# The first tile of pairs prepared inside an earlier stage, and the last chunk's reciprocal applied when attention loads it

## The chip, the cores and the metric

The kernel runs on one core of a Trainium2 chip. The core has a tensor engine (PE; its weight loads are a row of their own, PEld), a vector engine (DVE), a scalar engine (ACT), GpSimd (POOL) and SyncE (SP), which only issues transfers. [...] Matmuls read SBUF and write PSUM, which this kernel uses in eight banks of 128 x 512 values. The metric is the device time of one execution in microseconds, given as the median of several runs.

## The reference

Four graph layers run one after the other on x of 8 batches, 2048 nodes and 64 features. Each layer normalises x, applies ReLU, computes something on the graph and adds it to x. Only layer 0 and the beginning of layer 1 matter here. Layer 0, cut to its core (E is 64 hyperedges, called edges below; H says which node belongs to which):

```python
h = x @ W
alpha = softmax(where(H.T > 0, leaky_relu(h @ a_node), NEG))     # per edge, over its nodes
agg = einsum('ben,bnf->bef', alpha, h)
beta = sigmoid((h @ a_gn)[:, None, :] + (agg @ a_ge)[:, :, None])
all_he = elu(beta * h[:, None] + (1 - beta) * agg[:, :, None])   # per (edge, node) pair
deg = maximum(adj.sum(-1), 1.0)[:, None]
industry = einsum('nm,bmf->bnf', adj / deg, x @ W_ind)
coefs1 = softmax(where(H > 0, attn_scores(elu(agg)), NEG))       # per node, over its edges
g = einsum('bne,benf->bnf', coefs1, all_he)
pair = stack([industry, g], axis=2)
out = einsum('bnk,bnkf->bnf', softmax(attn_scores(pair)), pair)
```

with `attn_scores(f) = tanh(f @ fcW + fcb) @ av`. Layers 1 to 3 (masked attention over neighbours, three message steps, and a graph convolution with a weight per node) follow and are not touched. H is sparse: a node has one edge and a few more, so the pairs (edge, node) of 128 nodes fit into 512 slots.

## The kernel before

Two batches of 64 features share the 128 partitions, so there are four batch pairs p (NP = 4). Nodes come in 16 tiles of 128 (NT) or in four chunks of 512 columns (NCW). A planner orders each engine's queue at compile time: it plays the program through with its own estimates of durations and issues an instruction on its engine when what it waits for is ready and no earlier traced one is ready too. What goes through the helper `InOrder` (the names V, A and G for DVE, ACT and POOL), or through `kit.mm` while `kit.strict` is set, keeps the order in which it was written. Everything else may be moved ahead, over long distances too. Pools of tiles are stacked in memory in the order in which their tags are first used, and a tile in a reused place waits for the last reader of what lay there.

The stages of layer 0 are these.

**Normalisation and lists** (to about 69 us). `norm` makes the normalised x, `pairs` makes for each node its first slot and its count (`mid`, `width`) and for each edge its ranks (Q), and Y is the normalised x times `W_ind`.

**Industries** (about 69 to 241 us), `industry(c)` for four chunks. Sixteen node tiles of adj are streamed, two in one load `at` of 512 KB issued by POOL into a pool of six buffers. PE multiplies them into four accumulators `acc0` to `acc3`, eight matmuls per node tile. After each node tile one function of the list `units` is called, so that small work is spread among the matmuls: for each of the 16 tiles `begin`, `part` and `end` of `members` (features `hi` and `lo` stored to DRAM, sums per edge into `pg` and `pd`), then `table_1` to `table_5` (tables per edge: `tab`, `ntab`, `etab`, and the denominators `rden`) and `rows` and `biases` (a bias table for layer 3). DVE adds the loads up (`ds`, L945). At a chunk's end DVE copies two accumulators and ACT two (`ev`, L949), PE sums `ds` over the partitions (`deg`, L952), DVE takes the minimum, clamps, inverts (L954 to L958) and multiplies the four `ev` by the reciprocal (L960), and SP stores them to `ind_dram` (L961). The units' PSUM tiles share two banks under the tag `ph`, and their SBUF tiles share four buffers under the tag `ev`.

**Pairs** (about 241 to 409 us), a loop over j = 0 to 70; a tile i has four steps k. Each tile is prepared by seven functions:

- `nodes`: ACT takes |slot - mid|, POOL compares it with `width` and so makes `sT` (which node has which slot)
- `ranks` and `edges`: PE makes `px`, DVE compares it with `slot` and makes `oT` (which edge has which slot)
- `turn` and `turned`: PE transposes `sT` into `pts`, ACT copies it to S
- `shares` and `shared`: PE makes `pm` with twelve small matmuls from `hhi`, `hlo` (the stored features, loaded by `features`) and `etab`, ACT makes `be` and `wt` from it

The loop prepares tile i + 1 while tile i is worked on; tile 0 is prepared before the loop, at L1236. A step then runs `pairs_of` (PE: `pd` and `pa`), `mixed` (two DVE operations, one exponential on ACT), `weighed` (DVE, then a multiplication on POOL) and `gathered` (PE adds the slots back to nodes with S). `divided`, `back` and `done` finish a tile into `gT`.

**Attention between industry and g** (about 409 to 492 us), a loop over 16 chunks (p, c). `first(i)` loads `iv` from `ind_dram` and scores it, `second(i)` scores g, `differ`, `third` and `fourth` weigh the two and add the result to x1. The first batch pair's sums stay on chip in `xs`, and `first_neighbours`, a generator that is advanced in this loop, begins layer 1 with them. The `iv` loads have nine buffers and are not held in order. The stores of g to x1, 1 MB each, go out on POOL as accumulating transfers (L1373).

Of the kernel before, what the change touches and what calls it, by code (L numbers as in the profile page):

```python
# [16 lines left out]
P = 128  # L17
# [744 lines left out]
def layer0(kit, hn, x1_dram, open_early, late_tile, between):  # L762
# [20 lines left out]

    sP = ExitStack()
# [10 lines left out]
    def features(i):  # L795

        hi = lst.tile([P, B * F + 2 * B], FR, tag="hhi", name="hhi", bufs=3)
        lo = lst.tile([P, B * F + 2 * B], FR, tag="hlo", name="hlo", bufs=3)
        nc.gpsimd.dma_start(out=hi, in_=hi_dram[i].bitcast(FR))
        nc.gpsimd.dma_start(out=lo, in_=lo_dram[i].bitcast(FR))  # L800
        return hi, lo

    with ExitStack() as sA:
# [110 lines left out]
        with ExitStack() as s1:  # L914
            sp = s1.enter_context(tc.tile_pool(name="streamf", bufs=6, reuse_waits="tile"))
# [10 lines left out]
            def industry(c):  # L926
# [20 lines left out]
                ev = [sb.tile([P, CW], FP, tag="ev", name="ev", bufs=4) for p in range(NP)]  # L947
                for p in range(NP):
                    (nc.scalar.copy if p % 2 else nc.vector.tensor_copy)(ev[p], acc[p])  # L949
# [3 lines left out]
                rdeg = sb.tile([P, CW], FP, tag="rdeg", name="rdeg", bufs=1)  # L953
# [4 lines left out]
                nc.vector.reciprocal(rdeg, rdeg)  # L958
                for p in range(NP):
                    nc.vector.tensor_mul(ev[p], ev[p], rdeg)  # L960
                    nc.sync.dma_start(out=ind_dram[p, :, cols(c)], in_=ev[p])  # L961

            def members(i):
# [14 lines left out]
                def part(j):  # L978
# [19 lines left out]
                    if j == 1:  # L998
                        nc.sync.dma_start(out=hi_dram[i], in_=hi.bitcast(FP))
                        nc.sync.dma_start(out=lo_dram[i], in_=lo.bitcast(FP))  # L1000

# [93 lines left out]
            for i in range(NT):  # L1095
                begin_, part_, end_ = members(i)
                units += [begin_, part_] + ([last] if last else [])
                last = end_
            units += [last, table_1]
            units += [lambda: rows(0), lambda: None, table_2, lambda: rows(1)]  # L1100
            for c, step in enumerate((table_3, table_4, table_5)):
                units += [lambda c=c: biases(c), step] + ([lambda c=c: rows(c + 2)] if c < 2 else [])
            units += [lambda: biases(3)]
# [4 lines left out]
        loaded = [features(i) for i in range(2)]  # L1108
# [5 lines left out]
    with ExitStack() as s0:  # L1114

        hot = s0.enter_context(tc.tile_pool(name="s_hot", bufs=2, reuse_waits="tile"))
# [7 lines left out]
        ident_r = sb.tile([P, P], FR, name="ident_r", bufs=1)  # L1124
        nc.vector.tensor_copy(ident_r, ident)
        tiles = [{} for i in range(NT)]

        def nodes(i):

            d = tiles[i]  # L1130
            d["sT"] = hot.tile([P, SLOTS], FR, tag="sT", name="sT", bufs=3)
            tmp = hot.tile([P, SLOTS], FP, tag="tmp", name="tmp", bufs=1)
            A.activation(tmp, slot, AF.Abs, bias=mid[:, i : i + 1])
            G.tensor_scalar(d["sT"], tmp, width[:, i : i + 1], None, op0=OP.is_lt)

        def ranks(i):
            d = tiles[i]
            d["px"] = ps.tile([P, SLOTS], FP, tag="px", name="px", bufs=2)
            mm(d["px"], Q[:, i].rearrange("p h e -> p (h e)"), d["sT"], start=True, stop=True)

        def edges(i):

            d = tiles[i]
            d["oT"] = hot.tile([P, SLOTS], FR, tag="oT", name="oT")
            V.tensor_tensor(d["oT"], d.pop("px"), slot, op=OP.is_equal)

        def turn(i):
            d = tiles[i]
            d["pt"] = ps.tile([P, NB, P], FP, tag="px", name="pts", bufs=2)
            for k in range(NB):  # L1150
                mm(d["pt"][:, k, :], d["sT"][:, k * P : (k + 1) * P], ident_r, start=True, stop=True)

        def turned(i):
            d = tiles[i]
            d["S"] = sb.tile([P, NB, P], FP, tag="S", name="S", bufs=3)
            A.activation(d["S"], d.pop("pt"), AF.Copy)

        def shares(i):

            d = tiles[i]  # L1160
            d["hi"], d["lo"] = loaded.pop(0)
            d["pm"] = pm = ps.tile([P, NB, 2 * B], FP, tag="px", name="pm", bufs=2)
            for k in range(NB):
                ks = slice(k * P, (k + 1) * P)
                mm(pm[:, k, :], d["sT"][:, ks], d["hi"][:, B * F :], start=True, stop=False)
                mm(pm[:, k, :], d["sT"][:, ks], d["lo"][:, B * F :], start=False, stop=False)
                mm(pm[:, k, :], d["oT"][:, ks], etab, start=False, stop=True)

        def shared(i):
            d = tiles[i]  # L1170
            d["be"] = sb.tile([P, NB, B], FP, tag="be", name="be")
            d["wt"] = sb.tile([P, NB, B], FP, tag="wt", name="wt")
            pm = d.pop("pm")
            A.activation(d["be"], pm[:, :, 0:B], AF.Tanh, scale=0.5)
            A.activation(d["wt"], pm[:, :, B:], AF.Copy)
# [60 lines left out]
        for step in (nodes, ranks, edges, turn, turned, shares, shared):  # L1236
            step(0)
        nodes(1)
# [6 lines left out]
        for j in range(last + 7):  # L1245
# [8 lines left out]
            if 3 <= j < last + 3:  # L1254
                weighed(j - 3)
            if 5 <= j < last + 5:
                gathered(j - 5)
# [35 lines left out]
    with ExitStack() as s0:  # L1293
# [17 lines left out]
        def first(i):  # L1311
# [3 lines left out]
            ths[i] = scores(iv, 2.0)  # L1315
# [30 lines left out]

        first(0)
# [8 lines left out]
        for i in range(len(chunks) + 2):  # L1356
# [12 lines left out]
            if i > 4:  # L1369
                next(steps, None)  # L1370
# [705 lines left out]
```

## Time and profile before

| what | us |
|---|---|
| median of three runs | 2058.82 |
| lowest and highest | 2055.77, 2061.78 |
| the profiled execution | 2053.27 |
| its span, from the first to the last instruction | 2051.2 |
| PE busy | 1992.0 (97%) |
| DVE busy | 1184.3 (58%) |
| ACT busy | 454.4 (22%) |
| POOL busy | 291.4 (14%) |

The profile is of one execution. Its times are counted from the start of the span. A line of a group or of the timeline names the line of the program, the engine, the operation and the tile that is written and read; L630 is the helper of everything that is kept in order on DVE, ACT and POOL, and L726 is that of `kit.mm`, so these are told apart by their tiles. The chain of waits goes back from the last instruction to what released it, and so on; "issue" in it is time in which the engine waited for nothing that the profile shows. An engine with a q behind it is its sequencer, which issues transfers. PE's ends are modelled, and some matmul records are missing. The clock is the share of full speed that PE was granted.

### The profile page before, as it was taken

The numbers are of one execution on the slowest core, as the hardware profiler recorded it, in microseconds if no ns is written. First come the engines' busy times: TensorE is split into PE (matmuls) and PEld (weight loads), VectorE is DVE, ScalarE is ACT, GpSimd is POOL, SyncE is SP. The second block draws the span as 40 slices with busy tenths as digits, with TensorE's granted clock in tenths as the row PEclk, the third lists the DMA queues.
The fourth block names the chain that finished last, engine by engine and source line by source line (L and its number), as shares of the span: only waits on it lengthen the run. The fifth ranks groups of instructions, "written<-read, shape, count | busy, mean of one in ns | idle before, by whom it ended". The sixth has DMA issues, their size and how long they took to land.

```text
span 2051.2 us, 23618 instructions
## 1 busy us (share of the span) xinstructions
PE 1992.0 (97%) x9164; PEld 1153.7 (56%) x9164; DVE 1184.3 (58%) x1867; ACT 454.4 (22%) x859; POOL 291.4 (14%) x399
## 2 busy tenths in 40 slices
PE   7999899988999999999999999999999999999997
PEld 4777677623323232237774567665477745677653
DVE  6667399866888888873216552245622165522355
ACT  4321255474111111121120111211111211112100
POOL 0211187511000000000001110101100011101012
PEclk9999899999999999999999999999999999999998
DMA  6766173185011111204101012100021001121000
GB/s 172 207 192 189 59 249 113 36 228 107 27 47 37 47 32 42 52 11 111 57 21 29 24 42 67 47 15 24 23 68 57 21 22 30 42 67 46 8 15 12
DMA packets 84251, 138.17 MB, mean 67 GB/s; under 512 B 32752, under 2 KB 33008, under 8 KB 81456
## 3 DMA queue, kind: packets, MB, share of 16 engines
q1 hardware_dynamic: 65200, 83.86, 13.9%
q0 software_dynamic: 18928, 52.70, 10.5%
q8 instruction: 74, 1.21, 0.3%
q14 instruction: 49, 0.40, 0.1%
HBM read 102.64 MB, written 37.03 MB: 68 GB/s over the span
## 4 chain that ended last, share of the span: by engine, by line
PE 71%; issue 15%; POOL 4%; DVE 3%; DMA 3%; ACT 2%; SPq 0%; POOLq 0%; DVEq 0%; ACTq 0%
PE acc L726 28%; PE o L726 11%; PE dn L726 6%; PE u L726 6%; PE pd L726 3%; PE acc L940 3%; PE pgs L726 2%; PE var L726 2%; PE mean L726 2%; PE py L726 2%; POOL fold L1964 1%; DMA iv<-ind_dram 1%; PE pm L726 1%; POOL ot L1965 1%; PE ph L726 1%
## 5 line engine op out<-in xcount | busy, mean ns | idle before, releaser
L726 PE MATMUL acc<-aT,parts 128*128 128x512 f32 x1664 | 456.0, 419 | 0.0
L726 PEld LDWEIGHTS acc<-aT,parts 128*128 128x128 f32 x1664 | 307.8, 188 | 111.8 <-issue 49.4
L1952 DVE TENSOR_TENSOR pr<-u,embf 128x512 f32<-128x512 f32 x256 | 170.6, 687 | 139.0 <-PE u L726 132.3
L1571 DVE SCALAR_TENSOR_TENSOR pt<-R,wd,aT 128x1024 f32<-128x1024 f32 x192 | 236.3, 1277 | 18.4 <-PE dn L726 6.6
L726 PE MATMUL u<-W3f,y 64*128 64x512 f32 x1024 | 241.0, 589 | 0.0
L726 PE MATMUL o<-pt,hS 128*64 128x512 f32 x1024 | 236.4, 599 | 0.8 <-DVE pt L1571 0.6
L726 PEld LDWEIGHTS u<-W3f,y 64*128 64x128 f32 x1024 | 99.2, 187 | 120.6 <-issue 120.6
L726 PEld LDWEIGHTS o<-pt,hS 128*64 128x64 f32 x1024 | 68.0, 136 | 159.2 <-issue 150.2
L726 PE MATMUL u<-W3f,v 64*128 64x512 f32 x512 | 138.8, 619 | 0.0
L940 PE MATMUL acc<-at,Y 128*128 128x512 f32 x512 | 134.9, 408 | 1.7 <-DVE ev L949 1.7
L1964 POOL TENSOR_TENSOR fold<-fold 128x256 f32<-128x256 f32 x64 | 47.8, 747 | 548.2 <-DVE fold L1963 510.4
L726 PE MATMUL dn<-pt,vd 128*32 128x512 f32 x1024 | 123.1, 598 | 0.0
L1788 DVE TENSOR_TENSOR yb<-py,cb_f 128x512 f32<-128x512 f32 x32 | 22.1, 691 | 173.8 <-PE py L726 173.8
L940 PEld LDWEIGHTS acc<-at,Y 128*128 128x128 f32 x512 | 94.2, 192 | 24.8 <-issue 4.1
L726 PE MATMUL acc<-aTl,parts 128*128 128x512 f32 x384 | 103.1, 405 | 0.0
L1956 DVE TENSOR_TENSOR pr<-pr 128x512 f32<-128x512 f32 x128 | 88.1, 688 | 2.2
L1571 DVE SCALAR_TENSOR_TENSOR pt<-R,wd,aTl 128x1024 f32<-128x1024 f32 x64 | 79.8, 1281 | 11.4 <-PE dn L726 8.2
L726 PEld LDWEIGHTS acc<-aTl,parts 128*128 128x128 f32 x384 | 72.2, 188 | 21.5 <-issue 5.7
L1856 POOL TENSOR_TENSOR bq<-bq,xp 128x512 f32<-128x512 f32 x16 | 20.6, 1285 | 434.0 <-DVE xp L1854 395.1
L1938 ACT COPY xs<-px 128x128 f32<-128x128 f32 x64 | 17.1, 267 | 272.7 <-POOL ot L1966 210.2
L630 POOL TENSOR_TENSOR mix<-ex,wt 128x512 f32<-128x512 f32 x64 | 68.3, 1069 | 33.7 <-DVE ex L630 28.9
L726 PEld LDWEIGHTS dn<-pt,vd 128*32 128x32 f32 x1024 | 26.7, 108 | 80.8 <-issue 75.4
(322 smaller groups left out, 2723.0 us busy)
## 6 DMA issues: line engine op xcount, KB each, us to landing
at<-in_adjT POOLq DMA_DIRECT2D x32, 512.0 KB, 4.5
raw<-in_adjT SPq DMA_DIRECT2D x64, 256.0 KB, 3.3
aT<-in_adjT POOLq DMA_DIRECT2D x12, 1024.0 KB, 5.3
xp<-xd SPq DMA_DIRECT2D x45, 256.0 KB, 3.2
R<-r_dram SPq DMA_DIRECT2D x14, 512.0 KB, 3.7
hi_dram<-hi SPq DMA_DIRECT2D x16, 264.0 KB, 2.5
lo_dram<-lo SPq DMA_DIRECT2D x16, 264.0 KB, 3.4
hhi<-hi_dram POOLq DMA_DIRECT2D x16, 264.0 KB, 3.1
```

The lines of the kernel that those rows point to most:

```text
L630: self.tc.keep_in_program_order(getattr(self.engine, name)(*args, **kw))
L726: one = self.nc.tensor.matmul(*args, **kw)
L940: mm(acc[p], Y[h][:, m, p, :], at[:, k, :], start=m + h == 0, stop=m == NT - 1 and h == 1)
L1571: nc.vector.scalar_tensor_tensor(pt, R[b2], wd[:, m, b2 : b2 + 1], aT[m][:, s].bitcast(FP), op0=OP.max, op1=OP.mult)
L1788: nc.vector.tensor_tensor(yb, py, bias[:, None, :].to_broadcast([P, 4, P]), op=OP.add)
L1856: nc.gpsimd.tensor_add(bq, bq, xp)
L1938: nc.scalar.copy(xs.rearrange("p h f -> p (h f)"), px)
L1952: nc.vector.tensor_tensor(a, u[h], emb[:, i, 8 * w : 8 * w + 8, None].to_broadcast([P, 8, F]), op=OP.mult)
L1956: nc.vector.tensor_add(pr[h], pr[h], a)
L1964: nc.gpsimd.tensor_add(fold[:, :, 0:2, :], fold[:, :, 0:2, :], fold[:, :, 2:4, :])
L1965: nc.gpsimd.tensor_add(ot, fold[:, :, 0, :], fold[:, :, 1, :])
```

## The change

Three things are done.

First, the preparation of tile 0 and `nodes(1)` become units of the last chunk's industries. The seven functions move up in the program, before the industries. They take engines, PSUM bank and scratch tile from a dictionary `now`: among the industries these are the plain engines (which the planner may reorder), the banks of `ph` and the buffers of `ev`; in the loop they are the ordered engines and the stage's own pools. The tiles of the first preparation (`sT0`, `oT0`, S0, `sT1`, `be0`, `wt0`) and `ident_r` lie in the pool `list`, the others in the stage's pool; `spot` chooses, and the number of buffers of each is as before. The `at` stream has four buffers instead of six. `features(0)` is traced in the units of tile 4.

Second, the last chunk (`late`) is no longer multiplied by its reciprocals at the chunk's end. All four of its accumulators are copied by ACT, and its clamped degrees stay in a new tile `rlast`, which all chunks now use. Steps 1 to 4 of the pairs each invert 128 of its columns.

Third, attention's loads get a function of their own, `fetched`, called for three chunks ahead of the loop and for chunk i + 3 at the end of step i. For the four pieces of the last chunk it multiplies `iv` by `rlast`, in order on DVE.

The diff, without the moved bodies that stay the same:

```diff
+    rlast = w0.tile([P, CW], FP, name="rlast")
...
+    ident_r = lst.tile([P, P], FR, name="ident_r")
+    nc.vector.tensor_copy(ident_r, ident)
+    tiles, loaded, now = [{} for i in range(NT)], [], {}
+
+    def spot(name, i, n, dt, bufs, ahead):
+        k = i % bufs
+        return (lst if k < ahead else now["pool"]).tile([P, n], dt, tag=f"{name}{k}", name=name)
+
+    def nodes(i):
+        d = tiles[i]
+        d["sT"] = spot("sT", i, SLOTS, FR, 3, 2)
+        tmp = now["tmp"]()
+        now["A"].activation(tmp, slot, AF.Abs, bias=mid[:, i : i + 1])
+        now["G"].tensor_scalar(d["sT"], tmp, width[:, i : i + 1], None, op0=OP.is_lt)
...
-            sp = s1.enter_context(tc.tile_pool(name="streamf", bufs=6, reuse_waits="tile"))
+            sp = s1.enter_context(tc.tile_pool(name="streamf", bufs=4, reuse_waits="tile"))
...
+                late = c == NCW - 1
                 for p in range(NP):
-                    (nc.scalar.copy if p % 2 else nc.vector.tensor_copy)(ev[p], acc[p])
+                    (nc.scalar.copy if late or p % 2 else nc.vector.tensor_copy)(ev[p], acc[p])
...
-                rdeg = sb.tile([P, CW], FP, tag="rdeg", name="rdeg", bufs=1)
+                rdeg = rlast
...
-                nc.vector.reciprocal(rdeg, rdeg)
+                if not late:
+                    nc.vector.reciprocal(rdeg, rdeg)
                 for p in range(NP):
-                    nc.vector.tensor_mul(ev[p], ev[p], rdeg)
+                    if not late:
+                        nc.vector.tensor_mul(ev[p], ev[p], rdeg)
                     nc.sync.dma_start(out=ind_dram[p, :, cols(c)], in_=ev[p])
...
+                    if j == 1 and i == 4:
+                        loaded.append(features(0))
...
+            now.update(
+                V=nc.vector, A=nc.scalar, G=nc.gpsimd,
+                tmp=lambda: sb.tile([P, SLOTS], FP, tag="ev", name="tmp", bufs=4),
+                bank=lambda shape, name: ps.tile(shape, FP, tag="ph", name=name, bufs=2),
+            )
...
             units += [last, table_1]
-            units += [lambda: rows(0), lambda: None, table_2, lambda: rows(1)]
-            for c, step in enumerate((table_3, table_4, table_5)):
-                units += [lambda c=c: biases(c), step] + ([lambda c=c: rows(c + 2)] if c < 2 else [])
-            units += [lambda: biases(3)]
+            units += [both((rows, 0), (nodes, 0)), both((ranks, 0), (turn, 0)), table_2]
+            units += [both((rows, 1), (edges, 0), (turned, 0))]
+            units += [both((biases, 0), (nodes, 1)), table_3, both((rows, 2))]
+            units += [both((biases, 1)), table_4, both((rows, 3))]
+            units += [both((biases, 2), (shares, 0)), table_5, both((biases, 3), (shared, 0))]
...
-        loaded = [features(i) for i in range(2)]
+        loaded.append(features(1))
...
-        hot = s0.enter_context(tc.tile_pool(name="s_hot", bufs=2, reuse_waits="tile"))
+        hot = s0.enter_context(tc.tile_pool(name="s_hot", bufs=1, reuse_waits="tile"))
...
+        now.update(
+            V=V, A=A, G=G, pool=hot,
+            tmp=lambda: hot.tile([P, SLOTS], FP, tag="tmp", name="tmp", bufs=1),
+            bank=lambda shape, name: ps.tile(shape, FP, tag="px", name=name, bufs=2),
+        )
...
-        for step in (nodes, ranks, edges, turn, turned, shares, shared):
-            step(0)
-        nodes(1)
...
+            if 1 <= j < 5:
+                part = slice((j - 1) * P, j * P)
+                V.reciprocal(rlast[:, part], rlast[:, part])
...
-        def first(i):
+        def fetched(i):
             p, c = chunks[i]
             iv = ivs[i] = io.tile([P, CW], FP, tag="iv", name="iv")
             nc.sync.dma_start(out=iv, in_=ind_dram[p, :, cols(c)])
-            ths[i] = scores(iv, 2.0)
+            if c == NCW - 1:
+                V.tensor_mul(iv, iv, rlast)
+
+        def first(i):
+            ths[i] = scores(ivs[i], 2.0)
...
+        for i in range(3):
+            fetched(i)
         first(0)
...
+            if i + 3 < len(chunks):
+                fetched(i + 3)
```

## The prediction

> **What bounds the kernel now.** I read the page first: PE is busy 97% of the span, so a stage gains only where PE stands or runs at half clock. Then the chain of waits around the two places that the change touches. First the end of the industries (start us, us, what):
>
> ```profile
> 240.65 0.47 PE deg L952 x2
> ...
> 241.83 0.60 DVE rdeg L957
> ...
> 242.49 3.32 DVE rdeg L958
> 245.81 0.56 DVE oT L630
> ...
> 246.41 2.31 PE pm L726 x10
> ...
> 249.74 1.57 POOL sT L630
> ```
>
> After the last industry matmul the chain leaves PE: the 3.3 us reciprocal stands in DVE's queue ahead of `oT` of tile 0, PE's `pm` waits for `oT`, and tile 1's `sT` is made only then. The first `pd` of the pairs starts at 248.56, 7.5 us after `deg`. The table by stretches (us; busy us and instructions of PE, PEld, DVE, ACT, POOL; clock; DMA share, GB/s) shows what follows:
>
> ```profile
> 241.00:245.40 4.40, 1.15 (x8) 0.87 (x7) 4.32 (x5) 1.53 (x3) 1.56 (x1) 1.00 0.00 0
> 245.40:255.70 10.30, 8.84 (x28) 7.14 (x29) 6.80 (x11) 2.95 (x7) 3.65 (x3) 0.50 0.27 102
> 255.70:273.00 17.30, 17.30 (x85) 12.83 (x83) 16.03 (x26) 7.61 (x15) 12.99 (x15) 1.00 0.78 244
> ```
>
> PE had 1.15 us of work in 4.4, and then ran 10.3 us at clock 0.50. From 255.7 on it is full.
>
> Second, the chain at the start of attention (380 to 450 us):
>
> ```profile
> 411.88 20.93 DMA iv<-ind_dram
> 432.81 0.14 issue
> 432.95 1.14 PE pf L726 x4
> ```
>
> PE and then DVE wait for one load of 256 KB that takes 20.9 us. SP's queue shows why it went out late, POOL's what it met:
>
> ```profile
> 398.30 0.32 SPq L1314 DMA_DIRECT2D iv<-ind_dram  x1
> 408.18 1.76 SPq L1352 DMA_DIRECT2D xo<-in_xT  x4
> 410.04 5.33 SPq L1314 DMA_DIRECT2D iv<-ind_dram  x7
> ```
>
> ```profile
> 410.57 2.72 POOL L1373 DMA_DIRECT2D xd<-hn  x3 [3.95 <-ACT hn L630]
> ```
>
> Seven `iv` loads stand behind four `xo` loads, which SP's waits put down to PE `pgs` (9.4 us), the last read of S. Asked one issue at a time, chunks 0 to 8 take 2.9, 3.1, 6.1, 6.4, 10.6, 15.8, 20.9, 21.3 and 21.0 us to land: those issued after 410.57 queue with three accumulating stores of 1 MB. So `iv3` lands at 416.8, `iv6` at 432.8, `iv7` at 434.5.
>
> [...] its cold stretches are 3.4 us (211.3, 231.8, 416.1) or 10.2 us (245.4), each behind idle time or a run of tiny matmuls. [...]
>
> **The change, part by part.**
>
> *1. Tile 0's preparation leaves the seam.* `nodes`, `ranks`, `turn`, `edges`, `turned`, `shares`, `shared` for tile 0 and `nodes(1)` become units among the industries' matmuls. ACT (4 us busy in 210 to 220, 1 us in 220 to 230), POOL (idle from 203 to 242) and DVE (0.17 us in 214.7 to 231.8) have room. PE has none there: it pays `px` 0.23, `pts` 0.39, `pm` 1.24 (their shares in the steady chain), 1.86 us, later by that.
>
> *2. The reciprocal and four multiplications leave the seam.* On DVE only the minimum (0.60), the clamp (0.60) and the comparison (0.06) remain after `deg`: DVE is free at 242.45. The last chunk's four copies go to ACT: accumulators end at about 239.3, 239.8, 240.2 and 240.7, ACT takes 0.6 each, so it ends at 241.7; the accumulators' banks are next written by `pa` and `px` at about 242, banks 2 to 5 in that order, so nobody waits. Covered.
>
> *3. Quarter reciprocals in the pairs' steps 1 to 4.* 128 columns took 0.95 us at L1075 against 3.35 for 512; start to start 0.87. The first steps are then DVE's. One `mixed` is 1.39 (starts 260.21, 261.00, 261.60), a `weighed` 0.61, an `edges` 0.60. From 242.45 to the end of `mixed(4)`: 5 x 1.39 + 4 x 0.87 + 0.60 + 2 x 0.61 = 12.25, so 254.7. Then `pairs_of(6)` 0.93 and `gathered(1)` 0.86, and tile 2's `pm` starts at 256.5. Before:
>
> ```profile
> 263.57 1.24 PE pm L726 x12
> ```
>
> That is 7.1 earlier. The next period holds DVE work of 9.2 (4 x 2.0 and 1.2) against PE's 9.2 to 9.6, so the gain stays.
>
> *4. What takes it back.* The 1.86. The units' order is fixed by the planner at compile time and can't be read off; tile 0's `tmp` also takes one of four `ev` buffers, freed only as chunk 2's stores land (204.1 to 208.4), and `px` holds one of two `ph` banks that `table_2` needs. PE already stood 0.5 and 1.0 us there for `t` and `eT`. I charge 0.7 (0 to 3). `pm` beside `pn` lengthens a run of tiny matmuls: a further cold window costs 3.4/2 = 1.7; at 0.4, 0.7. Net of this seam: 7.1 - 1.9 - 0.7 - 0.7 = 3.8 (0.5 to 5.5).
>
> *5. Four buffers for `at` instead of six.* One load lasts PE about 5.2 us (POOL's issues are 4.6 to 5.3 apart) and lands in 4.0 to 7.2. With four, POOL issues when PE frees the buffer of four loads ago, three loads = 15.6 us ahead: 8 us in hand. What would be late first is `ds` on DVE, then the members' `lo` and `hs` queued behind it. Zero; without that cover up to 2 per chunk.
>
> *6. `features(0)` is traced earlier.* Its two POOL issues already went out at 79.84 and 80.52: zero.
>
> *7. Attention's loads.* `fetched(0..2)` come before `xo`. More weighty is where the buffers lie. I laid the pools out by the tags' order. `iv2` covers `rden`, last read by `gn` at 408.14 to 408.8, so it can't go before 408.85. In the kernel before, `xo` lies over S0, read by the last `pgs` till 408.1; in the new layout S0 sits in the list pool under the `th` buffers, and `xo` lies over `tmp`, oT1, S1, S2, `wt1`, free at 398.8 and 405.7 (end of POOL's last `mix`). As SP's order follows readiness, `xo` goes out at 399 and 405.7, `iv2` at 408.85, and at 0.43 each `iv3`, `iv4`, `iv5` by 410.2, ahead of the stores; `iv6` takes the place of `iv4`, about 421.5.
>
> Then, with PE's 0.96 per pair of `pf`, ACT's 1.05, DVE's rows: `first(2)` starts at 414.15 (its bank is free) not 416.31; `differ(0)` ends 415.4, the new multiplication of `iv3` 416.0, `differ(1)` starts 416.65 not 419.04; `differ(2)` 418.9 to 420.0. From there DVE sets the pace, `fourth` 2.06 + `second` 0.6 + `differ` 1.13 = 3.8 a chunk, plus 0.6 for `iv7`: `fourth(3)` ends at 434.1. Before, it ended at 437.91, PE having waited 2.30 us for `iv2`, 0.57 for `iv5` and 0.73 for `iv6`. Gain 3.8. The multiplications of `iv11` and `iv15` fall in DVE's idle times of 1.8 and 4.7 us: I charge 0.4. Net 3.4 (-1 to 4).
>
> The multiplications wait for a DMA, in order, on DVE: behind the one for `iv3` stand `second(2)`, `differ(1)` and `fourth(0)`; PE's `third(1)`, and through it the sums `xo` that layer 1's normalisation reads, wait for those. It costs only its 0.6 while `iv3` lands before 415.4.
>
> **Sum.** The profiled execution took 2053.27, its span is 2051.2, 2.1 lie around it. 3.8 + 3.4 = 7.2 off: 2046.1 for that execution. It stood 5.5 below the median of the three runs, 2058.82 (2055.77 to 2061.78), inside their scatter; I take the difference off the median: 2051.6.
>
> **Rivals.**
> *Seam alone*: SP keeps `xo` behind `iv2`, or the landings stay as they are and the multiplications fill idle DVE time. For it: `iv3` landed at 416.8 and DVE then waited till 418.43. Against: the layout above. 2058.8 - 3.8 = 2055.
> *The industries give it back*: `sT` or `px` of tile 0 comes late in PE's queue, or `at` comes late. PE stood only 4.3 us in all from 69 to 241, so the queue is tight; POOL's `sT` would share its queue with `at` issues that wait for PE. At the upper ends of part 4 (3 for order, 1.7 for the clock), and one buffer wait of 2, 8.6 with the 1.9: the seam is -1.5, with attention's 3.4 about 2057.
> *Slower, DVE held by `iv3`*: if `iv2` at 408.85 goes ahead of the four `xo`, `iv3` is issued near 411, behind the second or third accumulating store, and lands like the loads issued at 411.40 or 411.88: 427.2 or 432.8. `second(2)` moves from 418.43 to 427.8 or later: 9.4 lost less 3.8, 2064.4. It decides from a landing at about 422 on.
> *The change doesn't do what it says*: the reciprocals still run, quartered, so 3.5 us of DVE stay on the path; that is in part 3. If PE stays cold in those steps, `pm` of 2.3 and pairs of 1.7 add about 2: 2053.6.
>
> **How the numbers follow.** Both gains 0.55, spread 2048 to 2054; seam alone (with the cold PE) 0.22, 2053 to 2057; given back 0.11, 2055 to 2062; slower by `iv3` 0.12, 2062 to 2069. 0.3% is 6.2 us, about what this measurement tells from nothing: bounds at 2052.6 and 2065. Below the first lies nine tenths of the first case and little of the others, 0.5. Above the second lies two thirds of the last and a remainder for an order that I didn't foresee, 0.12. Between, 0.38. Range 2046.5 to 2062; the likeliest case alone 2048 to 2054.
>
> **What the new profile would show.** `pd` of pair 0 within 1 us after `deg`; no clock 0.50 for 10 us; tile 2's `pm` some 15 to 16 us after `deg` (22.9 before). `deg` itself 2 to 4 us later than 240.65. `xo` issued at 399 to 406, `iv3` landing before 415, no `iv` load on the chain. Wrong if PE waits for `sT`, `px` or `at` before `deg`, or if the multiplication at load time has a DMA wait before it.

## The result, and the profile after

The changed kernel takes 2063.61 us (2054.97 to 2070.55) against 2057.32 for the kernel before on the same chip: a ratio of 1.0032, 95% interval 1.0019 to 1.0044. The forecast was 2051.6, in a range up to 2062.0. The profiled execution took 2066.63, its span is 2064.8. It lies 3.0 above its median, and the profiled execution of before 4.0 below its own. So the two profiles differ by 13.4 us where the medians differ by 6.3, and the losses read off them below add up to more than the medians show.

The seam did what the prediction said. The chain of waits of the changed kernel around it (start us, us, what):

```profile
252.70 0.46 PE deg L1013 x2
253.16 0.69 PE pd L726 x3
...
255.93 0.86 DVE rlast L630
...
267.94 1.35 PE pm L726 x12
```

The pairs begin as `deg` ends, and tile 2's `pm` comes 15.2 us after `deg`; before, it was 22.9. From the end of `deg` to the start of the twenty-first `mixed` it is 48.5 us, 55.8 before: 7.3 gained where step 3 had 7.1. This does not hang on one profile: the stretch is 48.5 to 50.0 in all twelve later kernels with both parts of the change, and 55.8 to 59.0 in the three that have neither (e1, e12, e16). But `deg` itself ends at 253.2 and not at 241.1. Two stretches lost these 12 us, and attention lost more.

**First chunk.** The timeline of the changed kernel (start us, us, engine, line, operation, output <- input, count, and in brackets the idle time before it and what ended it):

```profile
86.31 0.53 POOL L801 DMA_DIRECT2D hhi<-hi_dram  x1 [5.77 <-DMA hi_dram<-hi]
86.98 0.53 POOL L802 DMA_DIRECT2D hlo<-lo_dram  x1
87.52 1.43 POOL L992 DMA_DIRECT2D at<-in_adjT  x2
...
94.89 1.23 DVE L1005 TENSOR_TENSOR ds<-ds,at 128x1024 fp32r<-128x1024 f32 x1 [5.32 <-DMA at<-in_adjT]
...
96.59 1.22 PE L1045 MATMUL ph<-W0x,hn 128*128 128x132 f32 x4 [3.61 <-DVE hs L1056]
```

Two block loads go out together at 87.5, because the first of them stood on POOL behind the features of tile 1, which waited 5.8 us for their rows to land. They land at 94.9 and 96.5. DVE's sum waits, `hs` is queued behind it, and PE waits 3.6 for `hs`. Before, a block load stood behind features too, but DVE's sum hardly waited:

```profile
92.78 0.55 POOL L799 DMA_DIRECT2D hhi<-hi_dram  x1 [3.50 <-DMA hi_dram<-hi]
...
94.01 0.70 POOL L932 DMA_DIRECT2D at<-in_adjT  x1
...
94.38 1.23 DVE L945 TENSOR_TENSOR ds<-at 128x1024 fp32r<-128x1024 f32 x1 [1.29 <-DMA at<-in_adjT]
```

The first eviction comes at 113.4 instead of 107.6. From the first industry matmul to it are 44.5 us, 38.1 before. Beside PE's wait, 6.8 of them are at half clock (95.0 to 101.8), which is 3.4 us of time; before, this chunk had none.

**Last chunk.** The table by stretches (us; busy us and instructions of PE, PEld, DVE, ACT, POOL; clock; DMA share, GB/s) of the changed kernel:

```profile
214.40:221.20 6.80, 6.80 (x17) 3.49 (x17) 4.55 (x5) 4.03 (x8) 2.19 (x1) 0.50 0.41 120
221.20:241.80 20.60, 20.60 (x114) 16.20 (x113) 2.12 (x4) 2.21 (x8) 0.74 (x1) 1.00 0.17 54
241.80:252.00 10.20, 10.20 (x22) 6.49 (x21) 0.53 (x1) 1.62 (x3) 0.00 (x0) 0.50 0.07 26
252.00:256.40 4.40, 4.40 (x22) 3.48 (x21) 3.10 (x6) 1.67 (x4) 0.57 (x1) 1.00 0.92 238
```

PE waits once, 1.6 us for tile 0's mask, just ahead of this table (timeline):

```profile
213.12 0.50 PE L726 MATMUL px<-sT,Q 128*128 128x512 f32 x1 [1.59 <-POOL sT L820]
```

From there it is busy throughout, but 17 us of the table are at half clock. In this chunk before they were 6.8:

```profile
211.30:214.70 3.40, 3.40 (x11) 2.29 (x8) 0.00 (x0) 2.11 (x5) 0.00 (x0) 0.50 0.26 87
...
231.80:235.20 3.40, 3.40 (x11) 2.80 (x11) 1.25 (x2) 0.00 (x0) 0.00 (x0) 0.50 0.00 0
```

From the third chunk's first eviction to the last chunk's it is 53.3 us, 47.0 before.

**Attention.** The timeline of the changed kernel:

```profile
390.00 25.10 SPq L1343 DMA_DIRECT2D iv<-ind_dram  x3
415.20 1.80 SPq L1387 DMA_DIRECT2D xo<-in_xT  x4
416.50 2.72 POOL L1410 DMA_DIRECT2D xd<-hn  x3 [4.98 <-ACT hn L630]
417.04 4.73 SPq L1343 DMA_DIRECT2D iv<-ind_dram  x6
433.14 0.69 DVE L630 TENSOR_TENSOR iv<-iv,rlast 128x512 f32<-128x512 f32 x1 [11.73 <-DMA iv<-ind_dram]
433.98 2.08 PE L726 MATMUL pf<-iv,fcWf 64*128 64x512 f32 x4 [10.33 <-DVE iv L630]
```

And its chain of waits there:

```profile
417.04 16.07 DMA iv<-ind_dram
433.12 0.02 issue
433.14 0.70 DVE iv L630
433.84 0.14 issue
433.98 3.78 PE pf L726 x8
```

SP's own waits from 380 to 430 (engine, line that waited, what for: us in total, times, longest):

```profile
SPq L1343 <- DVE gn L630: 11.2, 1, 11.2
```

The third load waits in SP's queue for the last division (`gn`), the four residual loads wait behind it, and the fourth, `iv3`, goes out after the first accumulating store. It lands at 433.1. The new multiplication waits 11.7 us for it in order, and PE stands 10.3. PE's clock is halved from 426.1 to 439.7, so its first work after that wait is slow too: four `pf` take 2.08 us there and 1.18 at 439.6.

### The profile page after: what moved, and what is told of

The parts are those of the page before. It is cut to its first block, busy times and chain, and to the rows that moved or that the text cites. A ratio compares the mean times of both kernels' runs of the same rounds, so it can differ in the third digit from the quotient of the medians.

```text
span 2064.8 us, 23613 instructions
## 1 busy us (share of the span) xinstructions
PE 2000.1 (97%) x9164; PEld 1155.5 (56%) x9164; DVE 1184.0 (57%) x1868; ACT 455.5 (22%) x861; POOL 291.7 (14%) x399
## 3 DMA queue, kind: packets, MB, share of 16 engines
q1 hardware_dynamic: 65200, 83.86, 13.7%
## 4 chain that ended last, share of the span: by engine, by line
PE 72%; issue 14%; POOL 4%; DVE 4%; DMA 2%; ACT 2%; POOLq 0%; SPq 0%; DVEq 0%; ACTq 0%
PE acc L726 28%; PE o L726 11%; PE dn L726 6%; PE u L726 6%; PE acc L1000 4%; PE pgs L726 3%; PE pd L726 2%; PE var L726 2%; PE mean L726 2%; PE py L726 2%; POOL fold L2001 1%; PE ph L726 1%; POOL ot L2002 1%; DMA at<-in_adjT 1%; PE pm L726 1%
## 5 line engine op out<-in xcount | busy, mean ns | idle before, releaser
L1000 PE MATMUL acc<-at,Y 128*128 128x512 f32 x512 | 139.3, 418 | 1.2 <-DVE ev L1010 1.2
L1975 ACT COPY xs<-px 128x128 f32<-128x128 f32 x64 | 17.1, 268 | 273.1 <-POOL ot L2003 210.6
```

The costliest lines, as they stand in the source:

```text
L1000: mm(acc[p], Y[h][:, m, p, :], at[:, k, :], start=m + h == 0, stop=m == NT - 1 and h == 1)
L1975: nc.scalar.copy(xs.rearrange("p h f -> p (h f)"), px)
```

## The experiments

A profile is one execution, and executions of one kernel differ by several us (2054.97 to 2070.55 in the changed one). So times are compared by medians and intervals, and profiles are read for where a wait is. Medians in us, with the kernel before on the same chip:

| kernel | median | before | ratio (95%) |
|---|---|---|---|
| e1 four block buffers alone | 2059.76 | 2057.01 | 1.0012 (1.0001 to 1.0024) |
| e2 preparation alone | 2056.74 | 2057.01 | 0.9994 (0.9982 to 1.0007) |
| e3 late multiplication alone | 2063.73 | 2057.01 | 1.0034 (1.0021 to 1.0046) |
| e4 change, residuals first | 2052.99 | 2057.01 | 0.9982 (0.9972 to 0.9993) |
| e5 change, features behind, all blocks in order | 2064.71 | 2058.14 | 1.0044 (1.0030 to 1.0059) |
| e6 e4 and e5 | 2055.29 | 2058.14 | 0.9994 (0.9981 to 1.0007) |
| e7 change, stores held | 2055.99 | 2058.14 | 0.9981 (0.9970 to 0.9993) |
| e8 e6, stores held | 2057.11 | 2058.14 | 0.9994 (0.9981 to 1.0007) |
| e9 e4, features behind | 2043.57 | 2056.04 | 0.9928 (0.9902 to 0.9955) |
| e10 e9, masks on VectorE | 2046.10 | 2056.04 | 0.9941 (0.9920 to 0.9963) |
| e11 e9, five block buffers | 2051.52 | 2056.04 | 0.9980 (0.9967 to 0.9992) |
| e12 e1, features behind | 2056.44 | 2057.82 | 0.9999 (0.9985 to 1.0012) |
| e13 e4 again | 2052.14 | 2057.82 | 0.9976 (0.9964 to 0.9988) |
| e14 e9 again | 2046.77 | 2057.82 | 0.9954 (0.9930 to 0.9977) |
| e15 e10 again | 2044.69 | 2057.82 | 0.9948 (0.9929 to 0.9966) |
| e16 before, features behind | 2059.47 | 2057.88 | 1.0004 (0.9987 to 1.0020) |
| e17 e9, two feature buffers | 2044.73 | 2057.88 | 0.9935 (0.9911 to 0.9959) |

e9, e10, e14, e15 and e17 rest on six to eight executions each, the others on 14 to 22. e1 to e4 share a chip, and so do e5 to e8, e9 to e11, e12 to e15, and e16 with e17; across such groups, only differences to the kernel before are compared.

My theory at the outset was: the queue's order in attention costs some 9 us, the four block buffers some 5, and the rest is the last chunk. The rival was that the multiplication on DVE and the stores' traffic cost attention its time whatever the order, and that the buffers are harmless.

### One part at a time

**e1**, the kernel before with

```diff
-            sp = s1.enter_context(tc.tile_pool(name="streamf", bufs=6, reuse_waits="tile"))
+            sp = s1.enter_context(tc.tile_pool(name="streamf", bufs=4, reuse_waits="tile"))
```

> The kernel before with four buffers for the blocks of the adjacency instead of six, and nothing else. Theory: the 5.3 us that the changed kernel lost in its first chunk come from the buffers alone: with four, the seventh load of a block stands on POOL's queue behind the two feature loads of tile 1, which wait for their rows to land. Then the first chunk's evictions come 4 to 6 us later than in the kernel before, the DVE sum waits about 5 us for a block near 90, and the whole is 4 to 6 us slower, near 2062.5. Rival: the buffers are harmless, as the prediction had it, and the hoisted feature load of tile 0 or the new memory layout made the wait: then no change, 2056 to 2058.5.

**e2**, the changed kernel without the late multiplication:

```diff
-                late = c == NCW - 1
+                late = False
...
-                V.reciprocal(rlast[:, part], rlast[:, part])
...
-        for i in range(3):
-            fetched(i)
```

without the loads at the end of a step, and with the load back in `first`.

> The changed kernel without the late multiplication: the last chunk takes its reciprocal and its four products where the kernel before took them, and attention loads its chunks as before. So only the moved preparation and the four buffers are left. Theory: the industries still lose 11 to 13 us (5 in the first chunk, 7 in the last), the seam gives back some 3.5 us, attention loses nothing: 7 to 10 us slower than before at the start of the attention, near 2065. Rival: the late multiplication is the cause of the whole loss, and the moved preparation pays: 2050 to 2056.

**e3**, the kernel before with the late multiplication: the lines that e2 takes out, put into it.

> The kernel before with the late multiplication alone: six buffers, the preparation of tile 0 in the seam as before, the last chunk unscaled, its reciprocal in quarters among the pairs, and attention's loads three ahead of the scores. Theory: the seam gains 3.5 to 4 us, and attention loses about 9 because its third load, which waits for the last division, is issued ahead of the four residual loads and the fourth lands some 15 us after issue behind the accumulating stores: 4 to 7 us slower, near 2062.5. Rival: the loads' order costs nothing once the pairs end at the old time, so only the seam's gain is left: 2053 to 2054.

**e4**, the changed kernel with the residual loads one place ahead:

```diff
-        for i in range(3):
+        for i in range(2):
             fetched(i)
+        for c in range(NCW):
+            xs.append(sb.tile([P, CW], FP, tag="x", name="xo", bufs=NCW))
+            nc.sync.dma_start(out=xs[c], in_=t["xT"][0, :, cols(c)])
+        fetched(2)
```

> The changed kernel with one thing moved: the four residual loads are issued between attention's second and third load, not behind the third. Theory: the queue's order was the cause in attention: the residuals go out near 413, the fourth load goes ahead of the first accumulating store and lands before 424, and 7 to 10 us of the changed kernel's time come back: 2054 to 2057, up to 3 us faster than or equal to the kernel before. Rival: the loss in attention comes from the product on VectorE and from the stores' traffic, whatever the order: no more than 2 us against the changed kernel, 2062 to 2065.

The late multiplication alone costs 6.7 us; with the residuals one place ahead the whole change, late multiplication included, is 4.0 us faster than before, where the changed kernel was 6.3 slower. That is 10.3 us between them, somewhat more than the 7 to 10 that I had expected. The timeline of e4:

```profile
385.67 13.48 SPq L1343 DMA_DIRECT2D iv<-ind_dram  x2
399.26 3.12 SPq L1384 DMA_DIRECT2D xo<-in_xT  x4
409.40 3.18 SPq L1343 DMA_DIRECT2D iv<-ind_dram  x7
411.11 2.72 POOL L1411 DMA_DIRECT2D xd<-hn  x3 [3.95 <-ACT hn L630]
415.90 0.68 DVE L630 TENSOR_TENSOR iv<-iv,rlast 128x512 f32<-128x512 f32 x1
```

`xo` goes at 399.3 to 402.0, `iv2` at 409.4 and `iv3` to `iv5` by 410.7, and the multiplication has no wait ahead of it. This is the order that step 7 had written down, and its place, with the residuals at 399 and `iv2` held until the last division, shows that the memory layout was read rightly; only the queue's order was not. (For e4 itself I had expected `xo` near 413.)

How long attention takes, from the last division to the last `differ`, follows how many loads are issued between that division and the first store. With one (`iv2`: the changed kernel and e3) it is 86.6 and 86.1 us, with two (before) 78.5, with four (e4 and e2) 73.9 and 73.5. The kernels further down fall into the same groups: one 86.3 (e5), two 77.5 to 82.8 (e16, e1, e12), four 73.0 to 76.6. Within a group they differ by up to 5.3 us. e7 and e8, whose stores are held, stand apart. In e2 nothing of attention's text is changed; the new layout alone lets the first `xo` out earlier, so that `iv2` to `iv5` are issued by 420.3, ahead of the first store at 420.7, and land by 426.6.

That is also why e2 missed its expectation (near 2065): its profiled execution ended the last chunk 12.5 us late, as expected, but got 2.6 back in the seam and 5.0 in attention, and its median is that of before. The median lies between theory and rival (2050 to 2056), which laid the whole loss on the late multiplication. By the medians that looks nearly right, as e3 loses as much as the whole change and e2 nothing; but in e2 a loss in the industries and gains behind it cancel. e3 gained only 0.5 us in the seam by the same measure (55.3 us), where I had expected 3.5 to 4. With both parts it is 7.3: each alone leaves the other's work on the chain. In e3 PE waits 2.6 us for tile 0's mask at 245.5; in e2 it waits 5.4 for DVE at 261.4, which had the 3.35 us reciprocal and the four multiplications first. Each of these two figures rests on one profile, so they are rough.

e1 lost 2.75 us, less than the 4 to 6 that I had expected, by the wait shown above. Its timeline has the same DVE sum:

```profile
95.00 1.23 DVE L945 TENSOR_TENSOR ds<-ds,at 128x1024 fp32r<-128x1024 f32 x1 [5.15 <-DMA at<-in_adjT]
```

### Hold what stands ahead

**e5**, the changed kernel with the features of tiles 0 and 1, and all blocks, through `InOrder` on POOL, so that they keep their written order.

> The changed kernel with the two first feature loads and all block loads kept in program order on POOL's queue, so that the features of tile 1 (and of tile 2, which follow them) are issued behind the last block of the industries and no block stands behind them. Theory: four buffers cost 2.7 us in the median only because a block load stood behind feature loads that waited for their rows; held back, no VectorE sum waits over 2 us for a block in the first chunk and 2 to 4 us come back: 2059.5 to 2061.5. Rival: four buffers are too few by themselves, since a block takes some 5 us from issue to landing: nothing comes back, 2063 to 2064.5.

**e6**, e4 with the same.

> The changed kernel with both repairs: the residual loads ahead of attention's third load, and the feature loads held behind the industries' blocks. Theory: the two losses are in different places and add, so 2 to 3 us below the kernel with the residual loads moved alone: 2049.5 to 2051.5. Rival: a first chunk that ends earlier is lost again in the last chunk, where the preparation's units wait for POOL and ScalarE at their own pace: no gain, 2052.5 to 2054.

**e7**, the changed kernel with its stores behind a read of the ninth load:

```diff
-            if i in (1, 4, 8):
-                p = 1 + i // 4
-                nc.gpsimd.dma_start(out=x1_dram[p], in_=gT[p], accum_op=OP.add)
+            if i == 5:
+                G = InOrder(tc, nc.gpsimd)
+                G.tensor_copy(seen, ivs[8][:, 0:1])
+                for p in range(1, NP):
+                    G.dma_start(out=x1_dram[p], in_=gT[p], accum_op=OP.add)
```

> The changed kernel with its loads in the changed order, but the three accumulating stores of the gathered rows held until the ninth load of the industries has landed (one element of it is read on POOL ahead of them). Theory: the late fourth load was late because the stores' packets went ahead of it, not because of its place in SP's queue: it lands within 5 us of its issue near 417, and 9 to 13 us come back: 2051 to 2055. Rival: the order in the queue or the product on VectorE holds the start of attention: less than 3 us come back, 2060.5 to 2063.5.

**e8**, e6 with the same.

> The changed kernel with all three: residual loads ahead of the third load, feature loads held behind the blocks, accumulating stores held until the ninth load has landed. Theory: with the residuals ahead four loads already land before the stores, so holding the stores adds little, 0 to 1.5 us on top of the two repairs: 2048.5 to 2051. Rival: the held stores are late for the second group's rows, which are read from the same memory, and cost 2 us or more: 2052 to 2056.

e5, e6 and e8, which all have it, missed, and the edit was to blame. The first chunk came back (38.2 us to the first eviction in all three), but the planner now put tile 0's mask ahead of the blocks, and the blocks could no longer pass it. The timeline of e5:

```profile
180.41 0.71 POOL L630 DMA_DIRECT2D at<-in_adjT  x1 [4.49 <-PE acc L1001]
207.60 2.15 POOL L821 TENSOR_SCALAR sT<-tmp,width 128x512 fp32r<-128x512 f32 x1 [26.48 <-ACT tmp L820]
209.71 1.48 POOL L630 DMA_DIRECT2D at<-in_adjT  x2
...
209.80 0.80 PE L726 MATMUL px<-sT,Q 128*128 128x512 f32 x1 [9.48 <-POOL sT L821]
```

POOL issued no block for 29 us, PE stood 9.5, and the last chunk took 66.3 us instead of 53.3, 30.7 of them at half clock. (The profiled execution of e5 lies 10.8 above its median, so the medians show less of this.) This is neither theory nor rival: the same kind of fault in another place.

e7 kept the changed order of loads and is 2.1 us under its kernel before, where the changed kernel was 6.3 above: 8.4 us came back, a little less than the 9 to 13 expected. Attention takes 79.2 us, 86.6 in the changed kernel. The timeline of e7:

```profile
416.80 1.80 SPq L1388 DMA_DIRECT2D xo<-in_xT  x4
418.64 4.14 SPq L1344 DMA_DIRECT2D iv<-ind_dram  x6
424.60 0.69 DVE L630 TENSOR_TENSOR iv<-iv,rlast 128x512 f32<-128x512 f32 x1 [1.59 <-DMA iv<-ind_dram]
443.41 2.72 POOL L630 DMA_DIRECT2D xd<-hn  x3
```

Its waits from 405 to 445 (engine, tile and line that waited, what for: us in total, times, longest):

```profile
POOL aTl L2044 <- PE pd L726: 29.6, 1, 29.6
ACT q L630 <- POOL seen L630: 3.5, 1, 3.5
```

So the multiplication costs 11.7 us of waiting when three stores of 1 MB are under way and 1.6 when they are not. The order matters because of the stores, and both must come together: the load of 256 KB that SP issued for it took 16.1 us beside POOL's stores (417.04 to 433.12, changed kernel) and some 6 without (418.64 to 424.60, e7). The held stores were late themselves, though, behind a load of layer 1 on POOL, and ACT waited 3.5 us for the read. In e8, where the residuals go first anyway, holding them gained nothing: attention 74.3 us, 74.2 in e6.

### The blocks' queue

**e9**, e4 with only the last block and the features of tiles 1 and 2 in order:

```diff
+        q = InOrder(tc, nc.gpsimd) if i in (1, 2) else nc.gpsimd
+        q.dma_start(out=hi, in_=hi_dram[i].bitcast(FR))
+        q.dma_start(out=lo, in_=lo_dram[i].bitcast(FR))
...
+                    end = c == NCW - 1 and g == NT // 2 - 1
+                    (InOrder(tc, nc.gpsimd) if end else nc.gpsimd).dma_start(
```

> The changed kernel with the residual loads ahead of attention's third load, and the feature loads of tiles 1 and 2 kept behind the last block load on POOL's queue; the blocks keep the planner's own order among themselves and against the masks of tiles 0 and 1, so that no mask holds a block as in the runs with all blocks in program order. Theory: the first chunk no longer waits for blocks behind feature loads, nothing is added in the last chunk, and 2 to 4 us come off the kernel with the residual loads moved alone: 2049 to 2051.5. Rival: the last chunk has its own cause (the PE clock halved around the tables' small products), and a shorter first chunk is worth little: 2052.5 to 2054.5.

**e10**, e9 with

```diff
-                V=nc.vector, A=nc.scalar, G=nc.gpsimd,
+                V=nc.vector, A=nc.scalar, G=nc.vector,
```

> As the kernel with the residual loads moved and the features of tiles 1 and 2 kept behind the blocks, and the two masks that are made among the industries' units computed on VectorE instead of POOL. Theory: PE's 1.6 us wait for the first mask in the last chunk and the half-clock window that begins with it go: the window near 212 falls from 6.8 us to 3.4 or less and 2 to 4 us come back in the last chunk: 2046.5 to 2049.5. Rival: the window near 212 comes from the units around it (the transposes and the bias product), not from the wait: the window stays and no more than 1 us comes back.

**e11**, e9 with `streamf` of five buffers, and two for `hhi` and `hlo`.

> As the kernel with the residual loads moved and the features of tiles 1 and 2 kept behind the blocks, with five buffers for the blocks instead of four; the room comes from the feature tiles, two of each instead of three, so that tile 2's features are loaded after tile 0's last pair. Theory: once nothing stands ahead of the blocks in the queue, four buffers carry the stream, and a fifth changes nothing: within 1.5 us of the kernel without it. Rival: the depth itself is short, the sums of VectorE still wait for blocks with four buffers, and a fifth gives 1.5 to 4 us.

**e12**, e1 with the features as in e9.

> The kernel before with four block buffers, the features of tile 0 loaded from the same unit as in the changed kernel, and those of tiles 1 and 2 kept behind the last block. Theory: the buffers cost only through the blocks that stood behind feature loads, so this is as fast as the kernel before, within 2 us: 2055.5 to 2059. Rival: the depth of four costs by itself and the time stays with the kernel with four buffers alone, 2.5 us or more over before: 2059.5 to 2062.

**e13, e14, e15**: e4, e9 and e10 on one chip.

> The changed kernel with the residual loads ahead of the third load, again, as the base of the two runs that follow on the same chip: 2052 to 2055 (2053.0 on the first chip).

> The same with the features of tiles 1 and 2 kept behind the last block. Theory of the queue: 2 to 4 us under the run with the residual loads moved alone. Rival, from the run with few executions: 8 us or more under it, which would need a second effect beyond the wait in the first chunk. Third: nothing, under 1.5 us, and the earlier number was a draw of the clock.

> The same with the two masks on VectorE. Theory: PE's wait for the mask in the last chunk is gone, and with it half of the half-clock window near 212: 1.5 to 4 us under the run with the features behind the blocks. Rival: within 1.5 us of it.

**e16**, the kernel before with the features as in e12 and its six buffers. **e17**, e9 with two feature buffers.

> The kernel before, with its six block buffers, the features of tile 0 loaded from the same unit as in the changed kernel and those of tiles 1 and 2 kept behind the last block. Theory: with six buffers a block stood behind feature loads for little (the issue near 94 waited some 3.5 us, with blocks in hand), so nothing changes: within 1.5 us of the kernel before. Rival: the kernel before paid for it too, and 3 us or more come off.

> The changed kernel with the residual loads ahead and the features of tiles 1 and 2 kept behind the blocks, four block buffers, and two feature buffers of each kind instead of three. Theory: the two feature buffers make tile 2's and later features late in the pairs and cost what the kernel with five block buffers cost: 2049 to 2053. Rival: they cost nothing, and it was the fifth block buffer: 2043.5 to 2048.

e12 speaks on the buffers: with four of them and no features in the way, the kernel before keeps its time (0.9999). Its interval overlaps that of e1, but its timeline shows the wait gone:

```profile
83.33 0.71 POOL L936 DMA_DIRECT2D at<-in_adjT  x1 [2.64 <-PE acc L944]
87.94 0.72 POOL L936 DMA_DIRECT2D at<-in_adjT  x1 [3.91 <-PE acc L944]
93.15 0.72 POOL L936 DMA_DIRECT2D at<-in_adjT  x1 [4.48 <-PE acc L944]
...
94.03 1.21 DVE L949 TENSOR_TENSOR ds<-ds,at 128x1024 fp32r<-128x1024 f32 x1 [0.59 <-issue]
```

Each block goes out when PE frees its buffer. With six buffers (e16, 1.0004) the features in the way cost nothing that can be measured: enough blocks were in hand. So neither the number of buffers nor the hoisted features alone is the cause, but the two together. The first chunk, to its first eviction, shows it best: 38.1 us in the kernel before and e16, 38.2 in e12 and e14, and 43.5 in e1, 44.5 in the changed kernel, where both meet.

In the change itself, e14 is 5.4 us under e13, more than the 2 to 4 expected; in the profiles it is 5.3 by the first eviction of the second chunk (147.8 and 153.1), of which 3.3 are the first chunk and most of the rest a half-clock window of 3.4 us at 113.4, in e13 only. e9 had shown a larger gap than that to e4, but against another chip.

Masks on VectorE (e15 against e14) gave 2.1 us less by the medians, e10 against e9 2.5 more: not settled. PE's wait for the mask did shrink, but the half-clock windows don't obey it. e14, timeline:

```profile
205.65 0.51 PE L726 MATMUL px<-sT,Q 128*128 128x512 f32 x1 [1.46 <-POOL sT L821]
```

and its stretches:

```profile
206.00:226.10 20.10, 20.10 (x98) 14.26 (x97) 7.06 (x8) 6.50 (x14) 4.03 (x5) 1.00 0.43 123
226.10:243.20 17.10, 17.10 (x54) 12.92 (x53) 1.24 (x2) 0.58 (x1) 0.00 (x0) 0.50 0.04 15
```

After that wait PE ran 20 us at full clock; in e15 the wait was 0.70 and a window came at 208.7 all the same. So this wait of some 1.5 us is neither enough for a window nor needed for one; that it begins the window, as I had it for the changed kernel, does not hold.

Five block buffers (e11) were 8 us slower than e9 on the same chip. e17 clears the feature buffers, which were the other half of that edit. Why a fifth block buffer should cost anything stays open. The two profiles agree within 1.5 us at the end of every stage, but that of e9 is the slowest of its six executions, so they don't show what the medians do. With half of the half-clock time taken off, e11's first chunk is 1.3 us longer and its last 1.8, where PE waits 2.95 us for tile 0's mask instead of 1.48.

The best version found is e9 with or without e10's edit: 0.5 to 0.7% faster than before, and so 0.8 to 1.0% faster than the changed kernel.

## Why the prediction was wrong

*Step 7, "As SP's order follows readiness", is the step that failed.* SP's queue kept the written order, as it does for the `iv` and `xo` loads in every profile here; a load that waited 11.2 us for the last division held four that were ready. The price was read rightly: the rival that is held by `iv3` was put at 2064.4 with the landing at 427.2 to 432.8, and measured are 2063.6 and 433.1. That the total agrees so well is in part luck: attention lost 8.1 us where the rival had 9.4, and the losses in the industries were larger than the rival counted. The rule was stated without evidence: the profile of before had shown one written order only, and no load on SP passing another. Why the planner moves none here, no run shows. With the order that the step assumed, e4 and e13 measure 2053.0 and 2052.1, and attention gains 4.6 us for the 3.4 of that step. That these medians lie so near the forecast of 2051.6 is luck: they still contain the fault of step 5.

*Step 5, "Zero", failed too.* The depth was argued from loads that go out as PE frees buffers. Step 6 looked at the features of tile 0, whose earlier place cost nothing (e12 and e16 have it); those of tiles 1 and 2 stand in the same queue, and the kernel before already showed them in the way, with waits of 1.4 us at 86.08 and 3.5 at 92.78 for rows to land. Alone it is 2.75 us (e1), in the change 5.4 (e13 less e14), half-clock time included.

*Step 4's working of the last chunk was right, its clock was not.* Take off half of the half-clock time, and the last chunk, counted between first evictions, lasts 43.6 us before, 43.4 in e1 and e12, and 44.2 in e16, where PE waits 2.35 us for a load; with the preparation in it, 45.5 in the changed kernel, 45.6 in e4, 45.2 in e13, 45.3 in e14 and 44.9 in e15. Against the first three that is 1.3 to 2.2 more, where the step said 1.86 for the work and 0.7 for the order. But half clock took 6.8 us of it before and 15.7 in the changed kernel, which is 4.4 us of time; I had charged 0.7, an estimate with a window of 3.4 us at half clock, as the one at 231.8 in the profile of before. Since e1 had 17.1 and e16 19.2 without any moved work, it can't be laid on the preparation. What the preparation is worth alone is not separated: e2 lies 3.0 us under e1, which has the same buffers, but it also has the new layout, and attention takes 73.5 us in it, 81.9 in e1.

*Steps 1 to 3* stand: 7.3 us for 7.1. With both obstacles gone the change is worth 11.0 us (e14 against the kernel before), where steps 3 to 7 had added up to 7.2. No step accounts for the excess: between the profiled executions it is 6.4 us, and that of before lay below its median.

Of the signs named, both that would prove it wrong came: the multiplication at load time had a DMA wait before it, and PE waited for `sT` before `deg`, 1.6 us at 213.1. Nor was the clock of 0.50 for 10 us gone; it had moved ahead of `deg` (241.8 to 252.0). That it would go with PE's idle time in the seam was my estimate from its place behind it (PE busy 1.15 us in the 4.4 before 245.4), and not shown by a run. `xo` went at 415, `iv3` landed at 433.1, and `deg` was 12 us late instead of 2 to 4.

## What to carry to other kernels

In these runs a queue that issues transfers was blocked by the first of them whose wait wasn't over: 11.2 us on SP and 5.8 on POOL in the changed kernel. When a load is moved, or a planner may move it, write down the queue's real order and ask of each place what it waits for and what stands behind it: the loss here came twice from ready transfers behind an unready one, on SP and on POOL, and once more from a mask when I tried to mend it (no block for 29 us in e5). Four buffers instead of six cost nothing while nothing in the issuing queue waited longer than the blocks in hand lasted (e12, 0.9999), and 2.75 us where something did (e1). And small loads that a chain needs had to be issued before the large stores, not merely early: `iv3`, issued 0.5 us after the first store, took 16.1 us to land.

## What the runs showed of the hardware

Three queues kept their order where it can be read. On DVE `oT` of tile 0 doesn't read the reciprocal of 3.3 us and had its `px` from PE by 244.2, but started as that reciprocal ended, at 245.8 (before). On SP the four residual loads went out from 415.20, behind an `iv` load that had waited 11.2 us, and on POOL two block loads went out at 87.52, behind feature loads that had waited 5.8 (changed kernel).

Half-clock time in the last chunk was 6.8 us in the kernel before, 10.2 in e3, 13.7 in e12, 17.1 in e1 and 19.2 in e16, with the same matmuls in that chunk and PE busy nearly throughout; two profiles of one kernel (e10 and e15) have 17.1 and 10.2. Half of the difference, up to 6 us, is time by which this one stage varied from profile to profile. The long window of e14, 17.1 us, began at 226.1, after twelve matmuls of 16 columns, with no wait of PE on record in the 20 us before it; e17 has the same window, from 225.4. The prediction read every window as standing behind idle time or a run of tiny matmuls, and these runs don't settle what begins one with PE busy.

Longer waits did go with windows. Between 70 and 120 us PE has ten waits of 2.0 to 3.6 us, in the changed kernel, e1 to e4, e7 and e13. At seven of them a half-clock window begins within 1.6 us of the wait's end; at three there is none (2.2 us in e3, 2.4 in e4, 3.1 in e13). The twelve kernels without such a wait have no window there.

The three accumulating stores of 1 MB each landed 5.6 us apart in the changed kernel (428.7, 434.3, 440.0), and of the loads issued from 417 on, just after the first, none landed before 433. The DMA engines were busy 0.96 of the time from 416.5 to 433.0, at 229 GB/s; from 400.0 to 416.5 it was 0.11 at 23, and the `iv` loads issued at 390.00 and 403.16 took 2.9 and 3.6 us.
